# Clearing scratch words on GpSimd between the row gathers of a graph layer

## The chip, the cores and the metric

The kernel runs on one core of one Trainium2 chip. The metric is the device time of one execution in microseconds (us). The kernel before takes 2163.11 us, the median of three runs (2162.38, 2163.11 and 2164.73).

Engines are named as the profile names them: PE is TensorE's matmul side and PEld its weight load, DVE is VectorE, ACT is ScalarE, POOL is GpSimd, SP is SyncE. A trailing q (POOLq, SPq) is the engine's sequencer, which reads the instructions and tests their waits.

## The reference

`x` is 12500 x 256 float32; `src` and `dst` are 200000 edges, sorted by `dst`. The layer is

```python
h   = maximum(layernorm(x), 0)
agg = segment_sum(h[src], dst, 12500)
z   = (1 + eps_gin) * h + agg
t   = relu(batchnorm(z @ W1 + b1))          # 256 -> 512
y   = relu(batchnorm(t @ W2 + b2 + h))      # 512 -> 256
out = x + y
```

Both batch norms take mean and variance over all 12500 nodes, so nothing of the second product can start before the first product of every node is done.

## The kernel before

The edges are cut into 1563 tiles of 128 (the last has 64), and the tiles into 131 groups of `GT = 12` (the last group has 3). The nodes are cut into 25 chunks of 512. The kernel holds two programs, `fast()` and `general()`, and chooses by a flag; with these inputs it runs `fast()`.

**The gathers.** For each tile of 128 edges one indirect DMA, issued by GpSimd at line 513 in `gather(i)`, fetches 128 rows of 256 float32 (1 KB each) by the row numbers in `srcT`. Groups 0 to 29 fetch from `x` and are normalised on chip; from `LEAD = 30` on they fetch from `h_tab`, the normalised table that the kernel has written to DRAM meanwhile. Groups 0 and 1 are gathered ahead of the loop at line 238. A group's twelve gathers are issued from its last tile to its first: `for t in reversed(range(t0, t0 + n))`.

**The step.** One pass of the loop at line 726 is a step. Step `i` issues `gather(i + AHEAD)` with `AHEAD = 3` on GpSimd, so that three further groups are under way while group `i` is consumed. On VectorE `edges` (line 545) builds the one-hot matrices of a group; on TensorE `sums(i)` (line 570) multiplies twelve gathered tiles with them into one 128 x 256 sum, `put` (line 635) places an earlier group's sum in its columns of `zc`, and `slice_of` (line 661) is a quarter of the first product for a chunk whose edges are all in. The matmuls of a step are tied together by `together`, so that TensorE raises its semaphore once for them all. The order is written out by hand; each engine runs its own instructions in that order and waits on semaphores for the others.

**What a gather waits for.** Completed gathers are counted on eight semaphores in turn, so gather `n` waits for the landing of gather `n - 8`. The first gather of a group also waits for TensorE's step, which frees the buffer it writes into. The sequencer carries that second wait as an event-semaphore instruction of its own.

**After the last gather.** GpSimd does four small subtractions (lines 870 to 873). The kernel then closes the last sums, merges the statistics (line 288), runs the second product (lines 915, 944 and 952), the second batch norm and the way out. In that part GpSimd has some additions on 128 x 1024 (lines 936, 1008, 1014), and no gather is left.

**Other work of GpSimd.** At the very start it clears four constants of one word a partition, `dstT` and `srcT` beyond their filled part (lines 204 and 205, 91 words a partition), and the scratch tile `first` (lines 224 and 225), and writes index ramps with `iota` (lines 103 and 232 to 234).

Of the kernel before, what the change touches and what calls it, by code (L numbers as in the profile page):

```python
# [8 lines left out]
F32 = mybir.dt.float32  # L9
# [6 lines left out]
P = 128  # L16
R = 4
EPS = 1e-5
GT = 12
# [17 lines left out]
def kernel(  # L37
# [16 lines left out]
    nc = tc.nc  # L54
    N, D = x.shape
# [77 lines left out]
    def slot(ga, t):  # L133
        return slots(ga, t)[:, 0, :]
# [209 lines left out]
    def fast():  # L344
# [24 lines left out]
        with ExitStack() as fs:  # L369
# [14 lines left out]
            with ExitStack() as es:  # L384
                ln = es.enter_context(tc.tile_pool(name="ln", bufs=2))
                ring = es.enter_context(tc.tile_pool(name="ring", bufs=RING))
                sel = es.enter_context(tc.tile_pool(name="sel", bufs=2))
# [17 lines left out]
                relative(dstT, start)  # L405
                nc.vector.tensor_scalar(shift, shift, row, None, op0=OP.add)

                moments, scaled = {}, {}

                def look(v, pairs, tag, k):  # L410
# [93 lines left out]
                def gather(i):  # L504
                    t0, n = groups[i]
                    k = i % (AHEAD + 1)
                    if i >= LEAD + AHEAD or k > AHEAD - RING:
                        ga = ((0, GT, ring.tile([P, GT, D], F32, name="gt")),)
                    else:
                        ga = early[k]  # L510
                    for t in reversed(range(t0, t0 + n)):
                        rows = left if t == full_tiles else P
                        nc.gpsimd.indirect_dma_start(  # L513
                            out=slot(ga, t - t0)[:rows], out_offset=None, in_=x if i < LEAD else h_tab,
                            in_offset=bass.IndirectOffsetOnAxis(ap=srcT[:rows, t : t + 1], axis=0),
                        )
                    gathered[i] = ga

                def span(i):
# [188 lines left out]
                for i in range(EARLY, min(AHEAD, NG)):  # L708
                    gather(i)
# [16 lines left out]
                for i in range(NG - CLOSE):  # L726
                    before = added
                    gather(i + AHEAD)
                    if 0 < i <= NCH:
                        turn(i - 1)  # L730
# [50 lines left out]
                for i in range(NG - CLOSE, NG + 1):  # L781
                    if i + AHEAD < NG:
                        gather(i + AHEAD)
# [558 lines left out]
    with tc.If(off == 0):  # L1342
        fast()
# [32 lines left out]
```

## Time and profile before

| | us |
|---|---|
| median of 3 runs | 2163.11 |
| the profiled execution, its own time | 2162.41 |
| its span | 2160.5 |
| POOL busy | 1553.6 (72%) |
| PE busy | 1633.1 (76%) |
| DVE busy | 784.2 (36%) |
| ACT busy | 499.8 (23%) |

The profile is one execution of the program. Its span runs from the first instruction to the end of the last; the profiled execution's own time is 1.9 us above the span and 0.7 us below the median.

Groups of instructions read: line, engine, operation, output tile `<-` input tiles, count `|` busy time in us, mean ns of one `|` idle time of the engine just before them and what ended most of it. "issue" stands for time in which the engine waited for nothing that the profile shows. A timeline row reads: start in us, duration in us, engine, line, operation, and in brackets the idle time before it with what ended it. A row of the windows reads: the stretch, its length, the busy time of PE, PEld, DVE, ACT and POOL with the count of instructions, the clock granted to TensorE as a share of full speed, the mean busy share of the 16 DMA engines, and the GB/s moved. A row of the waits reads: the waiting engine and line, what ended the wait, the total in us, how often, the longest.

### The profile page before, as it was taken

Reading aid. Unit: us, or ns where it says so; the run is one execution under the profiler, and the core shown is the slowest. Engines: PE = TensorE matmul, PEld = TensorE weight load, DVE = VectorE, ACT = ScalarE, POOL = GpSimd, SP = SyncE. Lnnn points to the kernel's source line nnn. Section 1 sums busy time; section 2 is a strip of 40 time slices with the busy share of each in tenths; the row PEclk is TensorE's granted clock in tenths of the full one; section 3 lists DMA queues with packets and bytes.
Section 4 is the critical chain, followed back from the end, with each engine's and each line's share of the span. In section 5 each row is a group of like instructions: output and inputs, shape, how many; then the busy total and the mean of one; then the engine's idle time right before and its main releaser. Section 6 shows DMA issues by size and latency. Waiting matters only on the chain.

```text
span 2160.5 us, 15155 instructions
## 1 busy us (share of the span) xinstructions
PE 1633.1 (76%) x4856; PEld 987.2 (46%) x4856; DVE 784.2 (36%) x1172; ACT 499.8 (23%) x947; POOL 1553.6 (72%) x1609
## 2 busy tenths in 40 slices
PE   2666776778877777777777777778777777889997
PEld 2554554554444434444444444434444444455445
DVE  6565666542122121221212212122122122126997
ACT  4766667530000000000000000000000000004555
POOL 7777777777777777777777777777777777774540
PEclk9778888887788788887888878888788897789999
DMA  6766776644444444444444344444444445456898
GB/s 185 232 214 213 248 224 206 200 134 120 125 130 121 122 130 120 129 124 120 130 125 134 114 125 133 117 124 125 124 130 130 115 127 160 124 169 206 309 321 329
DMA packets 146048, 349.48 MB, mean 162 GB/s; under 512 B 30696, under 2 KB 58468, under 8 KB 145958
## 3 DMA queue, kind: packets, MB, share of 16 engines
q0 software_dynamic: 75008, 204.90, 33.4%
q1 hardware_dynamic: 43088, 104.47, 13.8%
q10 hardware_dynamic: 27862, 39.03, 5.0%
q8 instruction: 41, 0.67, 0.1%
q14 instruction: 49, 0.40, 0.1%
HBM read 284.28 MB, written 64.00 MB: 161 GB/s over the span
## 4 chain that ended last, share of the span: by engine, by line
POOL 54%; issue 23%; PE 8%; DMA 7%; DVE 5%; ACT 3%; SPq 0%; DVEq 0%; ACTq 0%; POOLq 0%
POOL gt L513 52%; DMA gt<-in_x_dram,srcT 4%; PE one L915 2%; PE pr L915 2%; PE pq L915 2%; ACT gt L441 1%; DMA gta<-in_x_dram,srcT 1%; DVE oh L545 1%; DVE stg L417 1%; DVE stc L417 1%; DMA gt<-h_tab,srcT 1%; POOL gta L238 1%; POOL gta L513 1%; ACT ht L441 1%; PE ps L570 0%
## 5 line engine op out<-in xcount | busy, mean ns | idle before, releaser
L513 POOL DMA_INDIRECT gt<-h_tab,srcT x1191 | 1125.8, 945 | 362.8 <-issue 362.2
L570 PE MATMUL ps<-gt,oh 128*128 128x256 f32 x2856 | 1001.4, 480 | 342.1 <-DMA gt<-h_tab,srcT 323.1
L570 PEld LDWEIGHTS ps<-gt,oh 128*128 128x128 f32 x2856 | 576.9, 226 | 765.1 <-DMA gt<-h_tab,srcT 662.2
L675 DVE BATCH_NORM_STATS2 st<-ph 128x6 f32<-128x512 f32 x96 | 67.0, 698 | 910.7 <-PE ph L661 910.7
L513 POOL DMA_INDIRECT gt<-in_x_dram,srcT x252 | 238.2, 945 | 76.8 <-issue 70.4
L621 ACT COPY zs<-ps 128x256 f32<-128x256 f32 x129 | 47.3, 367 | 804.9 <-PE ph L661 550.3
L545 DVE TENSOR_TENSOR oh<-col,dstT 128x1536 f32<-128x1536 f32 x129 | 225.1, 1746 | 0.0
L661 PE MATMUL ph<-zc,w1s 128*128 128x512 f32 (+1 forms) x392 | 206.3, 655 | 14.7 <-DVE hc L498 13.2
L681 ACT COPY ts<-ph 128x512 f32<-128x512 f32 x96 | 56.2, 586 | 590.3 <-DVE st L675 584.8
L651 DVE TENSOR_TENSOR zc<-pz,zc 128x512 f32<-128x512 f32 (+7 forms) x185 | 90.9, 517 | 258.1 <-PE pz L635 258.1
L635 PE MATMUL pz<-at,zs 128*128 128x256 f32 x516 | 170.7, 465 | 3.2 <-DVE zc L651 1.9
L635 PEld LDWEIGHTS pz<-at,zs 128*128 128x128 f32 x516 | 125.9, 245 | 31.2 <-ACT zs L621 5.2
L441 ACT ACTIVATE gt<-gt,nbg,rsg 128x256 f32<-128x256 f32 x252 | 126.1, 586 | 24.8 <-DVE nbg L435 24.8
L484 PE MATMUL ph<-ident,ht 128*128 128x128 f32 x196 | 44.0, 379 | 110.8 <-ACT ht L441 81.7
L661 PEld LDWEIGHTS ph<-zc,w1s 128*128 128x128 f32 x392 | 87.6, 225 | 83.9 <-issue 60.4
L417 DVE BATCH_NORM_STATS2 stg<-gt 128x6 f32<-128x512 f32 x126 | 84.4, 696 | 101.5 <-DMA gt<-in_x_dram,srcT 101.2
L484 PEld LDWEIGHTS ph<-ident,ht 128*128 128x128 f32 x196 | 31.1, 191 | 131.3 <-ACT ht L441 89.4
L513 POOL DMA_INDIRECT gta<-in_x_dram,srcT x56 | 52.9, 945 | 17.0 <-ACT gt L441 6.7
L626 DVE TENSOR_SCALAR at<-col,shift 128x256 f32<-128x256 f32 x129 | 61.2, 476 | 0.0
L936 POOL TENSOR_TENSOR ax<-ax,by 128x1024 f32<-128x1024 f32 x10 | 23.9, 2393 | 48.6 <-ACT by L893 44.7
L441 ACT ACTIVATE ht<-xt,nbc,rsc 128x256 f32<-128x256 f32 x98 | 50.5, 585 | 0.0
L570 PE MATMUL ps<-gtb,oh 128*128 128x256 f32 x80 | 31.9, 567 | 22.7 <-ACT gtb L441 22.2
(188 smaller groups left out, 1077.2 us busy)
## 6 DMA issues: line engine op xcount, KB each, us to landing
t_tab<-ts ACTq DMA_DIRECT2D x96, 256.0 KB
gt<-h_tab,srcT POOLq DMA_INDIRECT x1191, 2.8
xt<-in_x_dram SPq DMA_DIRECT2D x24, 512.0 KB
h_tab<-ht ACTq DMA_DIRECT2D x24, 512.0 KB
h_cols<-hc SPq DMA_DIRECT2D x24, 512.0 KB
zc<-h_cols SPq DMA_DIRECT2D x24, 512.0 KB
yT<-h_cols SPq DMA_DIRECT2D x24, 512.0 KB
ax<-t_tab SPq DMA_DIRECT2D x11, 512.0 KB
```

Of the source, the lines that this page charges most:

```text
L417: nc.vector.bn_stats(st[:, c : c + 2, :].rearrange("p c s -> p (c s)"), two.rearrange("p c d -> p d c"),)
L441: nc.scalar.activation(slot(to, c), slot(v, c), AF.Relu, bias=nb[:, c : c + 1], scale=rs[:, c : c + 1])
L484: nc.tensor.transpose(ph[:, c * P : (c + 1) * P], ht[:, c, d * P : (d + 1) * P], ident)
L513: nc.gpsimd.indirect_dma_start(out=slot(ga, t - t0)[:rows], out_offset=None, in_=x if i < LEAD else h_tab, in_offset=bass.IndirectOffsetOn ...
L545: nc.vector.tensor_tensor(ohs[i][:, :n, :], col[:, :P].unsqueeze(1).to_broadcast([P, n, P]), dstT[:, t0 : t0 + n].unsqueeze(2).to_broadcas ...
L570: nc.tensor.matmul(ps, lhsT=oh[:rows, j, :], rhs=slot(ga, j)[:rows], start=(j == order[0]), stop=(j == order[-1]))
L626: nc.vector.tensor_scalar(ats[i][:, :n], col[:, :n], shift[:, i : i + 1], None, op0=OP.is_equal)
L635: nc.tensor.matmul(pz[:, d, :n], lhsT=zs[:, d * P : (d + 1) * P], rhs=at[:, :n], start=True, stop=True)
L651: nc.vector.tensor_add(side, pz[:, :, a - lo : b - lo], side)
L661: nc.tensor.matmul(ph[:, :n], lhsT=w1s[:, d, f * P : (f + 1) * P], rhs=zc[c][:, d, :n], start=(d == 0), stop=(d == DC - 1),)
L675: nc.vector.bn_stats(st1[:, f, c, :], ph[:, :n])
L915: nc.tensor.matmul(ps, lhsT=w[:, k, :], rhs=t[:, k, :], start=(k == 0), stop=(k == DC - 1))
```

## The change

A scratch tile `gap` of 2048 float32 a partition is added. In 70 of the 131 groups GpSimd clears some of its words right after a gather, in five stretches of 14 groups each. Nothing reads `gap`.

| groups | words a partition | after which gathers | clearings |
|---|---|---|---|
| 50 to 63 | 83 | every one | 168 |
| 64 to 77 | 180 | every one | 168 |
| 78 to 91 | 327 | every one | 168 |
| 92 to 105 | 512 | tiles 8, 4 and 0 of the twelve | 42 |
| 106 to 119 | 2048 | tile 0, the last issued | 14 |

```diff
+                gap = sel.tile([P, 8 * D], F32, name="gap", bufs=1)
+                breaks = {}
+                for i0, long, every in ((50, 83, 1), (64, 180, 1), (78, 327, 1), (92, 2 * D, 4), (106, 8 * D, GT)):
+                    for i in range(i0, i0 + 14):
+                        breaks[i] = long, every
+
                 moments, scaled = {}, {}
...
                             out=slot(ga, t - t0)[:rows], out_offset=None, in_=x if i < LEAD else h_tab,
                             in_offset=bass.IndirectOffsetOnAxis(ap=srcT[:rows, t : t + 1], axis=0),
                         )
+                        if i in breaks and (t - t0) % breaks[i][1] == 0:
+                            nc.gpsimd.memset(gap[:, : breaks[i][0]], 0.0)
                     gathered[i] = ga
```

In the built program these are 560 clearings. Each but the first waits on GpSimd's own semaphore for the clearing before it, since both write the same words. No gather gets a new wait. The instructions of the other engines and their order are the same, but for one: a late load into `yT`, issued by SP, also waits for GpSimd, because that tile takes over the place of `gap`.

## The prediction

> **What bounds the kernel now.** I read the page first (chain and groups), then the waits and the windows of the loop's middle, then GpSimd's timeline at three places.
>
> ```profile
> span 2160.5 us, 15155 instructions
> ...
> POOL 54%; issue 23%; PE 8%; DMA 7%; DVE 5%; ACT 3%; SPq 0%; DVEq 0%; ACTq 0%; POOLq 0%
> ...
> L513 POOL DMA_INDIRECT gt<-h_tab,srcT x1191 | 1125.8, 945 | 362.8 <-issue 362.2
> ```
>
> The chain that ended last is POOL for 54% and "issue" for 23%. The group says that this issue time is GpSimd's own: between two gathers it is idle for 362.8 / 1191 = 0.305 us and waits for nothing that the profile names. A gather is 0.945 + 0.305 = 1.25 us. The waits from 800 to 1800 us agree:
>
> ```profile
> POOL gt L513 <- issue: 243.7, 800, 0.3
> POOL gt L513 <- DMA gt<-h_tab,srcT: 0.3, 1, 0.3
> ...
> PE ps L570 <- DMA gt<-h_tab,srcT: 237.3, 343, 2.5
> ```
>
> Of 800 gathers one waited for a landing, and none for TensorE to free a buffer. TensorE waits for gathers, 237.3 us of these 1000. So whatever GpSimd loses here is not made up by others: everyone else is waiting for it already.
>
> ```profile
> 40.00:400.00 360.00, 236.62 (x906) 185.07 (x907) 223.67 (x408) 243.73 (x511) 272.28 (x289) 0.82 0.69 217
> ...
> 1036.00:1246.00 210.00, 157.74 (x436) 89.66 (x435) 44.77 (x57) 12.95 (x26) 158.82 (x169) 0.84 0.42 123
> ...
> 1957.00:2160.50 203.50, 186.70 (x596) 99.91 (x594) 175.64 (x227) 107.30 (x143) 74.32 (x34) 0.97 0.83 300
> ```
>
> The second row stands for the changed stretches: 210 us hold 14 groups of 12 gathers, PE is busy 157.7 of them, the DMA engines 42%. The third is the part behind the last gather, 203.5 us in which nothing is gathered.
>
> ```profile
> 1953.23 0.90 POOL L513 DMA_INDIRECT gt<-h_tab,srcT  x1 [0.30 <-issue]
> 1954.44 0.95 POOL L513 DMA_INDIRECT gt<-h_tab,srcT  x1 [0.31 <-issue]
> 1955.70 0.95 POOL L513 DMA_INDIRECT gt<-h_tab,srcT  x1 [0.30 <-issue]
> 1958.84 0.72 POOL L870 TENSOR_TENSOR mix<-w2s 128x256 f32<-128x256 f32 x1 [2.19 <-PE ps L613]
> ```
>
> The gathers run from 3.21 us to 1956.65 us (1955.70 + 0.95) at an even 1.25 us, 1563 of them, and everything behind hangs on the last. A microsecond added between gathers is a microsecond on the end.
>
> **The change, part by part.** It removes nothing. It adds 168 + 168 + 168 + 42 + 14 = 560 clearings on GpSimd, and their waits.
>
> *The price of a clearing.* None stands between gathers before; the nearest rows are GpSimd's clearings at the start.
>
> ```profile
> 0.24 0.10 POOL L1362 MEMSET const-float32-0.0<- 128x1 f32 x1 [0.24 <-issue]
> 0.27 0.11 POOL L1362 MEMSET const-float32-1.0<- 128x1 f32 x1
> 0.30 0.12 POOL L1362 MEMSET const-bfloat16-1.0<- 128x1 bf16 x1
> 0.33 0.12 POOL L1362 MEMSET const-uint8-127<- 128x1 uint8 x1
> 0.85 0.23 POOL L103 IOTA jp<- 128x128 int32 x1 [0.40 <-POOLq L1362]
> 1.02 0.17 POOL L204 MEMSET dstT<- 128x91 f32 x1
> 1.14 0.17 POOL L205 MEMSET srcT<- 128x91 int32 x1
> 1.25 0.28 POOL L224 MEMSET first<- 128x128 f32 x1
> 1.49 0.24 POOL L232 IOTA place<- 128x131 int32 x1
> 1.67 0.19 POOL L225 MEMSET first<- 1x128 f32 x1
> 3.21 1.10 POOL L238 DMA_INDIRECT gtb<-in_x_dram,srcF  x1 [0.97 <-DMA srcF<-in_src_dram]
> 4.62 0.95 POOL L238 DMA_INDIRECT gtb<-in_x_dram,srcE  x1 [0.30 <-issue]
> 5.87 0.95 POOL L238 DMA_INDIRECT gtb<-in_x_dram,srcE  x1 [0.30 <-issue]
> ```
>
> These rows overlap each other (0.24 + 0.10 lies beyond 0.27), so I count from end to end, which is what the engine is held for. The one-word clearings end at 0.34 and 0.45, three steps apart: 0.037 us each. The two of 91 words end at 1.31, behind the ramp that ends at 1.08: 0.115 us each. That makes 0.037 us plus (0.115 - 0.037) / 90 = 0.867 ns a word. The 128-word clearing of one partition took 1.86 - 1.73 = 0.13 us, where the line gives 0.148. That one waited for the clearing of `first` with a ramp in between, much as the new ones wait, and shows no surcharge. So 83 words cost 0.109 us, 180 words 0.193, 327 words 0.320, 512 words 0.481 and 2048 words 1.812. The last two are far beyond the rows; at the 0.73 ns a word of the one-partition clearing the long ones would cost 0.411 and 1.53 us.
>
> Taken by the durations of the rows (0.1125 us for one word in the mean of four, 0.17 us for 91, so 0.64 ns a word), the five are 0.165, 0.227, 0.321, 0.439 and 1.42 us, and the sum below would be 168 x 0.713 + 42 x 0.439 + 14 x 1.42 = 158 us instead of 150. The Trainium skill, page "Perfetto Trace Analysis", section "GPSIMD Engine Instruction", says to distrust a GpSimd row's span and to time by the spacing of consecutive instructions; the overlapping rows here agree, and I go by the spacing.
>
> *Is the clearing hidden by something?* The candidate is the 0.305 us between gathers. If that were the sequencer making the next gather ready, the cores would stand still and could clear meanwhile. Sequencer rows speak against it (860 to 880 us, with the first gathers of a group):
>
> ```profile
> L513 POOLq EVENT_SEMAPHORE  x1: 17/17/17, 866.0 to 866.0; - x1
> ...
> DMA to landing us min/median/max: 2.7/2.8/4.4
> ```
>
> ```profile
> 873.30 0.95 POOL L513 DMA_INDIRECT gt<-h_tab,srcT  x1 [0.30 <-issue]
> 874.55 0.95 POOL L513 DMA_INDIRECT gt<-h_tab,srcT  x1 [0.30 <-issue]
> 875.80 0.95 POOL L513 DMA_INDIRECT gt<-h_tab,srcT  x1 [0.30 <-issue]
> ```
>
> The gather at 873.30 is number 1 + (873.30 - 4.62) / 1.25 = 696, counted from 0, which is 58 x 12, the first of group 58. It alone of its group has the extra wait, and the sequencer tested that at 866.0, 7.3 us or six gathers earlier. So gathers stand ready long before their turn, and the 0.305 us belongs to the engine's own work on a gather. Clearings then add in full. I take that, and keep the hidden case as a rival.
>
> *The waits of the clearings.* A clearing waits for the one before it, with at least one gather between. Behind it on the sequencer stand the next gathers, so the lead of six shrinks to about one. One is enough: the gather ahead holds the cores for 1.25 us, and the earlier clearing ended before that gather began. I cost this at 0; without that cover each of the 559 waits would show as part of a gather's 1.25 us. The gathers' own waits gain slack: eight gathers take 10 us or more against landings of 2.8 (4.4 at most), and TensorE frees its buffers relative to a slower pace.
>
> *VectorE beside it.* The 128-word clearing of 128 partitions took 1.53 - 1.31 = 0.22 us, 0.07 more than the line. VectorE was busy at that moment. In the stretches VectorE is busy 44.8 of 210 us: if every clearing met it by that share, 560 x 0.21 x 0.07 = 8 us. I leave that in the range.
>
> *The wait of SP.* One `yT` load waits for the last clearing, which lies 11 groups, some 150 us, before the last gather; these loads come behind the gathers. Cost 0.
>
> *The sum.* 168 x (0.109 + 0.193 + 0.320) + 42 x 0.481 + 14 x 1.812 = 104.5 + 20.2 + 25.4 = 150 us. The profiled execution would be 2162.4 + 150 = 2312.4 (span 2310.5); the median is 0.7 above it, so I forecast 2313 us. What is late next: nothing new, TensorE only waits longer. Its lower load might raise the granted clock, but behind the gathers that stands at 0.97, so at most 3% of 186.7, 5.6 us, could be won there.
>
> **The rivals.**
>
> *The gap hides them.* If the cores really rest in the 0.305 us, 83 and 180 words are free, 327 cost 0.015, 512 cost 0.176 and 2048 cost 1.507: 168 x 0.015 + 42 x 0.176 + 14 x 1.507 = 31 us, or 2194. For it: the profile can't name the gap. Against it: the lead of six gathers.
>
> *A gather behind a clearing starts cold.* The first gather, the only one behind other GpSimd work, took 1.10 instead of 0.95, and the next followed 1.41 us after it instead of 1.25. If each of 560 gathers paid 0.16, that is 90 more: 2403. For it: that row. Against it: it was also the first gather of all, and no later row separates the two.
>
> *The pace is the transfers'.* If the DMA path, not GpSimd, set 1.25 us, GpSimd would have slack in every gather, clearings up to it would be free, and after a long one it would catch up: 2163, not slower. The point that decides is whether a gather still follows 1.25 us after the one before in the first stretch. For it: the 64-row gather (the row at 1953.23) held its place for 1.21 us, hardly less than one of 128. Against it: the pace is the same with the DMA engines at 69% (40 to 400 us) and at 42%, and one gather's landing takes 2.8 us with several in flight. With a higher clock behind the gathers on top this could even end some us faster.
>
> That the clearings aren't carried out is hardly open: all 560 stand in the program.
>
> **How the numbers follow.** Full cost 0.72; cold restarts 0.12; hidden in the gap 0.11; pace of the transfers 0.05, of which 0.01 faster. The forecast is the first case, 2313. Its own range is 2285 to 2340: the cheaper slope takes 42 x 0.07 + 14 x 0.28 = 7 us off, a hidden 0.037 us per clearing another 21; VectorE adds 8, and the 158 us of the durations as much again. The range of 8 in 10 takes in the cold restarts and leaves the two hidden cases out: 2280 to 2403. Slower by over 0.2% (4.3 us, about what a measurement of this kernel can tell from no change) holds all but the last case: slower 0.95, same 0.04, faster 0.01.
>
> **What the changed profile would show.** GpSimd's timeline should have gathers 1.36, 1.44 and 1.57 us apart in the first three stretches, in the fourth 1.25 with 1.73 across each clearing, in the fifth 1.25 with 3.06; the five stretches 228, 242, 264, 230 and 235 us long instead of 210. TensorE's waits for gathers should grow by as much, and the part behind the last gather stay near 203.5 us. A spacing of 1.25 in the first two stretches shows the gap or the transfers at work, and the long clearing tells them apart: followed by gathers closer than 1.25, it is the transfers. Gathers of 1.10 behind clearings show the cold restart. The prediction is wrong as a whole if the long clearings' slope is far from 0.87 ns, or if the shrunken lead lets gathers wait by name.

## The result and the profile after

The changed kernel takes 2276.73 us (median of three runs, 2276.61 to 2276.80) against 2163.11 before: a ratio of 1.0524, 95% interval 1.0500 to 1.0548. It is 113.6 us slower. The forecast was 150 us more, with a range that began at 2280. The direction and the place were right; the price of one clearing was too high.

The page of the changed kernel, its chain and its groups on GpSimd (`gather` is now at line 519, the clearing at 524):

```profile
span 2274.9 us, 15716 instructions
...
POOL 63%; issue 18%; PE 8%; DMA 5%; DVE 3%; ACT 2%; POOLq 0%; ACTq 0%; DVEq 0%
...
L519 POOL DMA_INDIRECT gt<-h_tab,srcT x1191 | 1129.8, 949 | 286.1 <-issue 285.2
...
L524 POOL MEMSET gap<- 128x83 f32 (+4 forms) x560 | 188.7, 337 | 0.3
```

The chain has more of POOL and less of "issue". The clearings are 188.7 us of busy time, but the idle time before the gathers fell from 362.8 to 286.1 us. The 560 clearings took a part of that idle time, and this is most of the miss. In the timeline one sees it at a single clearing of the first, third and fifth stretch:

```profile
759.97 0.95 POOL L519 DMA_INDIRECT gt<-h_tab,srcT  x1 [0.16 <-issue]
760.92 0.18 POOL L524 MEMSET gap<- 128x83 f32 x1
761.27 0.95 POOL L519 DMA_INDIRECT gt<-h_tab,srcT  x1 [0.16 <-issue]
...
1441.06 0.95 POOL L519 DMA_INDIRECT gt<-h_tab,srcT  x1 [0.17 <-issue]
1442.01 0.38 POOL L524 MEMSET gap<- 128x327 f32 x1
1442.56 0.95 POOL L519 DMA_INDIRECT gt<-h_tab,srcT  x1 [0.17 <-issue]
...
1697.13 0.95 POOL L519 DMA_INDIRECT gt<-h_tab,srcT  x1 [0.30 <-issue]
1698.38 0.95 POOL L519 DMA_INDIRECT gt<-h_tab,srcT  x1 [0.30 <-issue]
1699.32 1.82 POOL L524 MEMSET gap<- 128x2048 f32 x1
1701.31 0.95 POOL L519 DMA_INDIRECT gt<-h_tab,srcT  x1 [0.17 <-issue]
```

A clearing begins as the gather ends, with no gap. Behind it the next gather starts after 0.165 us, not after the 0.305 that stand between two gathers (0.30 in the last stretch, where two gathers adjoin). So 0.14 us of the gap stand between two gathers alone. The rows of the five sizes, by their forms, give the clearing's own length:

```profile
L524 POOL MEMSET gap<- 128x327 f32 x168 | 65.0, 387 | 0.1
...
L524 POOL MEMSET gap<- 128x180 f32 x168 | 44.4, 265 | 0.1
L524 POOL MEMSET gap<- 128x83 f32 x168 | 30.9, 184 | 0.1
...
L524 POOL MEMSET gap<- 128x2048 f32 x14 | 25.5, 1825 | 0.0
...
L524 POOL MEMSET gap<- 128x512 f32 x42 | 22.8, 543 | 0.0
```

That is 0.115 us plus 0.833 ns a word (0.387 - 0.184 over 244 words). The 0.14 us cover the 0.115 and 0.025 more; against that, the gather behind a clearing shows a longer row, 0.952 us in place of 0.946. Together this is 0.115 - 0.140 + 0.006 = -0.019 us for each clearing, beside its words. What is left on the path is seen in the spacing of gathers, start to start, as the median of a stretch; beside it what the stretches lengthened by:

| words, after which gathers | spacing without / with a clearing, us | one clearing costs | forecast | stretch longer by | forecast |
|---|---|---|---|---|---|
| 83, each | 1.250 / 1.299 | 0.049 | 0.109 | 8.8 | 18.3 |
| 180, each | 1.250 / 1.380 | 0.130 | 0.193 | 22.1 | 32.4 |
| 327, each | 1.250 / 1.502 | 0.252 | 0.320 | 43.1 | 53.8 |
| 512, every fourth | 1.250 / 1.650 | 0.400 | 0.481 | 17.1 | 20.2 |
| 2048, every twelfth | 1.250 / 2.930 | 1.680 | 1.812 | 23.6 | 25.4 |

The five points lie on one line, 0.833 ns a word less 0.019 us, within 0.008 us; divided by the number of clearings, the stretches lie within 0.004 us of it. So the distance between clearings does not seem to enter. The stretches sum to 114.7 us and the span grew by 114.4.

The windows of the changed kernel, the five stretches and the part behind the last gather:

```profile
753.47:972.33 218.86, 161.33 (x437) 92.67 (x436) 45.49 (x60) 13.63 (x27) 190.50 (x337) 0.83 0.42 121
972.33:1204.44 232.11, 180.98 (x436) 101.45 (x436) 45.36 (x58) 14.57 (x28) 204.12 (x336) 0.74 0.39 112
1204.44:1457.58 253.14, 192.10 (x433) 101.96 (x433) 44.82 (x58) 13.98 (x27) 224.59 (x336) 0.70 0.36 104
1457.58:1684.62 227.04, 175.28 (x436) 98.23 (x437) 45.49 (x60) 13.63 (x27) 181.73 (x210) 0.77 0.41 117
1684.62:1918.16 233.54, 172.55 (x436) 93.03 (x435) 44.76 (x57) 13.98 (x27) 184.33 (x183) 0.80 0.39 111
2071.40:2274.90 203.50, 187.12 (x598) 100.37 (x596) 176.18 (x227) 107.40 (x143) 74.20 (x35) 0.97 0.83 301
```

The last row is as before: 203.5 us, clock 0.97. Nothing was won or lost behind the gathers.

### The profile page after: what moved, and what is told of

The parts are those of the page before. It is cut to its first block, busy times and chain, and to the rows that moved or that the text cites. A ratio compares the mean times of both kernels' runs of the same rounds, so it can differ in the third digit from the quotient of the medians.

```text
span 2274.9 us, 15716 instructions
## 1 busy us (share of the span) xinstructions
PE 1713.9 (75%) x4856; PEld 1023.0 (45%) x4856; DVE 784.5 (34%) x1172; ACT 499.8 (22%) x947; POOL 1744.7 (77%) x2169
## 4 chain that ended last, share of the span: by engine, by line
POOL 63%; issue 18%; PE 8%; DMA 5%; DVE 3%; ACT 2%; POOLq 0%; ACTq 0%; DVEq 0%
POOL gt L519 53%; POOL gap L524 8%; DMA gt<-in_x_dram,srcT 3%; PE one L923 2%; ACT gt L447 2%; PE pr L923 2%; PE pq L923 2%; DMA gta<-in_x_dram,srcT 1%; DVE oh L553 1%; POOL gta L519 1%; ACT ht L447 1%; PE pq L952 1%; POOL gta L238 1%; DVE stg L423 1%; DVE stc L423 0%
## 5 line engine op out<-in xcount | busy, mean ns | idle before, releaser
L519 POOL DMA_INDIRECT gt<-h_tab,srcT x1191 | 1129.8, 949 | 286.1 <-issue 285.2
L578 PE MATMUL ps<-gt,oh 128*128 128x256 f32 x2856 | 1058.2, 501 | 378.3 <-DMA gt<-h_tab,srcT 360.6
L578 PEld LDWEIGHTS ps<-gt,oh 128*128 128x128 f32 x2856 | 598.5, 236 | 836.3 <-DMA gt<-h_tab,srcT 733.8
L519 POOL DMA_INDIRECT gt<-in_x_dram,srcT x252 | 238.2, 945 | 76.8 <-issue 71.3
L669 PE MATMUL ph<-zc,w1s 128*128 128x512 f32 (+1 forms) x392 | 213.7, 675 | 15.5 <-DVE hc L504 13.9
L524 POOL MEMSET gap<- 128x83 f32 (+4 forms) x560 | 188.7, 337 | 0.3
L643 PE MATMUL pz<-at,zs 128*128 128x256 f32 x516 | 184.6, 496 | 3.2 <-DVE zc L659 1.9
L643 PEld LDWEIGHTS pz<-at,zs 128*128 128x128 f32 x516 | 133.4, 259 | 34.4 <-ACT zs L629 5.5
L669 PEld LDWEIGHTS ph<-zc,w1s 128*128 128x128 f32 x392 | 92.6, 238 | 89.6 <-issue 63.9
L519 POOL DMA_INDIRECT gta<-in_x_dram,srcT x56 | 52.9, 945 | 17.1 <-issue 8.2
L944 POOL TENSOR_TENSOR ax<-ax,by 128x1024 f32<-128x1024 f32 x10 | 23.6, 2361 | 46.7 <-ACT by L901 39.7
```

The costliest lines, as they stand in the source:

```text
L519: nc.gpsimd.indirect_dma_start(out=slot(ga, t - t0)[:rows], out_offset=None, in_=x if i < LEAD else h_tab, in_offset=bass.IndirectOffsetOn ...
L524: nc.gpsimd.memset(gap[:, : breaks[i][0]], 0.0)
L578: nc.tensor.matmul(ps, lhsT=oh[:rows, j, :], rhs=slot(ga, j)[:rows], start=(j == order[0]), stop=(j == order[-1]))
L643: nc.tensor.matmul(pz[:, d, :n], lhsT=zs[:, d * P : (d + 1) * P], rhs=at[:, :n], start=True, stop=True)
L669: nc.tensor.matmul(ph[:, :n], lhsT=w1s[:, d, f * P : (f + 1) * P], rhs=zc[c][:, d, :n], start=(d == 0), stop=(d == DC - 1),)
```

## The experiments

All spacings below are medians of gather starts in the trace, without a stretch's first and last group. The first four kernels ran on one chip beside the kernel before (2166.13 us there); each replaces the five stretches by eight of ten groups, groups 40 to 119.

**How small may a clearing be?**

```diff
-                for i0, long, every in ((50, 83, 1), (64, 180, 1), (78, 327, 1), (92, 2 * D, 4), (106, 8 * D, GT)):
-                    for i in range(i0, i0 + 14):
-                        breaks[i] = long, every
+                for k, long in enumerate((1, 8, 16, 24, 36, 48, 64, 128)):
+                    for i in range(40 + 10 * k, 50 + 10 * k):
+                        breaks[i] = long
...
+                        if i in breaks:
+                            nc.gpsimd.memset(gap[:, : breaks[i]], 0.0)
```

> One clearing after every gather, in eight stretches of ten groups (groups 40 to 119) of 1, 8, 16, 24, 36, 48, 64 and 128 words a partition. The changed kernel's five stretches lie on one line: a clearing lengthens the spacing of two gathers by 0.833 ns a word minus 0.019 us. Theory of room: beside a gather there are 0.056 us in which a clearing runs free, and the clearing itself is 0.037 us plus 0.833 ns a word; then the spacing stays at 1.250 us for 1, 8 and 16 words and grows by 0.001, 0.011, 0.021, 0.034 and 0.088 us for the others; together 120 x 0.155 = 19 us. Rival, replacement: a gather that follows another instruction is 0.019 us shorter than one that follows a gather, so the line goes on below zero: 1 word -0.018 us, 8 words -0.012, 16 words -0.006, and the others as above; together 120 x 0.119 = 14 us, and the kernel with one word everywhere would be the fastest. Rival, the prediction's own: 0.037 us at one word, 0.144 at 128.

| words | 1 | 8 | 16 | 24 | 36 | 48 | 64 | 128 |
|---|---|---|---|---|---|---|---|---|
| spacing, us | 1.251 | 1.257 | 1.257 | 1.257 | 1.257 | 1.264 | 1.277 | 1.333 |

The kernel takes 2184.64 us, 18.5 more than before. GpSimd's rows at 24 and at 128 words:

```profile
1119.98 0.95 POOL L519 DMA_INDIRECT gt<-h_tab,srcT  x1 [0.17 <-issue]
1120.92 0.14 POOL L524 MEMSET gap<- 128x24 f32 x1
1121.23 0.95 POOL L519 DMA_INDIRECT gt<-h_tab,srcT  x1 [0.17 <-issue]
...
1732.53 0.95 POOL L519 DMA_INDIRECT gt<-h_tab,srcT  x1 [0.16 <-issue]
1733.48 0.22 POOL L524 MEMSET gap<- 128x128 f32 x1
1733.86 0.95 POOL L519 DMA_INDIRECT gt<-h_tab,srcT  x1 [0.16 <-issue]
```

There is a floor. One word is free, and from 8 to some 36 words a clearing costs 0.006 us, by which the gather behind it shows a longer row (0.952 in place of 0.946). Replacement falls: one word does not shorten the spacing, and 8 and 16 words lengthen it. The prediction's price falls too: it makes 120 x 0.578 = 69 us of these 325 words. The theory of room holds in kind, but its sizes are off by 0.004 to 0.007 us, too low from 8 to 24 words and too high from 36 on, so that its sum of 19 us meets the 18.5 in part by luck. The time alone could not tell 19 from 14: both kernels ran once on this chip, and three runs of the kernel before lie 2.4 us apart.

**Is the room there once for each gap?**

```diff
+                gaps = [sel.tile([P, 2 * D], F32, name=f"gap{k}", bufs=1) for k in range(4)]
+                for k, longs in enumerate(((180,), (90, 90), (60, 60, 60), (45, 45, 45, 45), (1, 1), (1, 1, 1, 1), (180, 1), (1, 180))):
...
+                        for gap, long in zip(gaps, breaks.get(i, ())):
+                            nc.gpsimd.memset(gap[:, :long], 0.0)
```

> The clearing after each gather cut up, each piece in a tile of its own, in eight stretches of ten groups: 180 words; 2 x 90; 3 x 60; 4 x 45; 2 x 1; 4 x 1; 180 and 1; 1 and 180. Room once for each gap between gathers (0.056 us, each clearing 0.037 us plus 0.833 ns a word): spacing grows by 0.131, 0.168, 0.205, 0.242, 0.020, 0.094, 0.169 and 0.169 us. Rival, a clearing has no fixed cost at all and the words alone count, less 0.019 us once: 0.131 in the first four, 0 in the two with single words, 0.131 to 0.132 in the last two.

| pieces | 180 | 2 x 90 | 3 x 60 | 4 x 45 | 2 x 1 | 4 x 1 | 180, 1 | 1, 180 |
|---|---|---|---|---|---|---|---|---|
| spacing, us | 1.380 | 1.413 | 1.439 | 1.472 | 1.251 | 1.296 | 1.413 | 1.408 |

The kernel takes 2294.69 us. A further clearing in the same gap costs 0.026 to 0.033 us beside its words. So a clearing has a fixed price, somewhat below the 0.037 forecast, and the room is there once for each gap: the rival without a fixed price falls. The two stretches of single words do not fit the theory: with two the spacing is 1.251, as the fallen rival had it, where 1.270 was expected, and with four 1.296, where 1.344 was. In the trace a further single word starts 0.028 us after the one before, as dear as a further clearing elsewhere and not the 0.038 of the theory, so that two of them just fit the room. With four, the next gather starts 0.151 us behind the last and not 0.163; why stays open.

**Which partitions hold GpSimd?**

```diff
+                for k, part in enumerate(((0, 128, 512), (0, 32, 512), (32, 64, 512), (64, 128, 512), (0, 1, 512), (64, 128, 1024), (64, 128, 2048), (0, 128, 1024))):
...
+                            p0, p1, long = breaks[i]
+                            nc.gpsimd.memset(gap[p0:p1, :long], 0.0)
```

> One clearing after every gather over a part of the partitions, in eight stretches of ten groups: partitions 0 to 127 x 512 words, 0 to 31 x 512, 32 to 63 x 512, 64 to 127 x 512, partition 0 x 512, 64 to 127 x 1024, 64 to 127 x 2048, 0 to 127 x 1024. If the engine is held by the instruction whatever its partitions: 0.41 us more spacing in the first five, 0.83, 1.69 and 0.83 in the others. If only the cores that prepare a gather are held, and these own low partitions: 0.41, 0.41, about 0, about 0, 0.41, about 0 for 1024 words, and for 2048 words, which are longer than a gather's 1.25 us, a spacing of about 1.75 set by the clearings themselves (0.5 more); 0.83 in the last.

| partitions x words | 0-127 x 512 | 0-31 x 512 | 32-63 x 512 | 64-127 x 512 | 0 x 512 | 64-127 x 1024 | 64-127 x 2048 | 0-127 x 1024 |
|---|---|---|---|---|---|---|---|---|
| spacing, us | 1.657 | 1.657 | 1.657 | 1.657 | 1.625 | 2.083 | 2.937 | 2.084 |

```profile
1698.63 0.95 POOL L519 DMA_INDIRECT gt<-h_tab,srcT  x1 [0.16 <-issue]
1699.57 0.98 POOL L525 MEMSET gap<- 64x1024 f32 x1
1700.71 0.95 POOL L519 DMA_INDIRECT gt<-h_tab,srcT  x1 [0.16 <-issue]
```

The kernel takes 2806.64 us. The engine is held by the instruction, whatever its partitions. The Trainium skill, page "GPSIMD Engine Reference", section "2.1 Instruction dispatch", says that each core begins the next instruction once its own share is done, and section "4. When to use GPSIMD" that one pair of cores prepares a DMA. From these one could hope that clearing partitions 64 to 127 leaves that pair free. These runs show no such thing: 64 partitions cost what 128 do, and so do partitions 0 to 31 and 32 to 63. These three parts share no partition, so whichever pair it is, one of them holds none of it. Only one partition alone is cheaper, by 0.032 us.

**Waits, distance, and other instructions.**

```diff
+                gaps = [sel.tile([P, D], F32, name=f"gap{k}", bufs=1) for k in range(7)]
+                ramp = sel.tile([P, D], I32, name="ramp", bufs=1)
+                for k, kind in enumerate((("one", 1), ("seven", 1), ("ramp", 1), ("one", 2), ("one", 3), ("one", 6), ("one", 12), ("copy", 1))):
...
+                                nc.gpsimd.memset(gaps[t % 7][:, :180], 0.0)
...
+                                nc.gpsimd.iota(ramp[:, :180], pattern=[[1, 180]], base=0, channel_multiplier=0)
...
+                                nc.gpsimd.tensor_copy(gaps[1][:, :180], gaps[0][:, :180])
```

> 180 words a partition in eight stretches of ten groups: cleared in one tile after every gather; in seven tiles in turn, so that a clearing waits for one seven gathers back; an index ramp in place of the clearing; the clearing after every 2nd, 3rd, 6th and 12th gather; a copy from one scratch tile to another after every gather. If the waits between clearings cost nothing, the first two are alike, 0.131 us more spacing. If the price of a clearing does not depend on the distance, each costs 0.131 us at every distance. If the saving belongs to the gather that follows anything else, ramp and copy show the same one: their own words' time less about 0.02 us (0.83 to 1.0 ns a word: 0.13 to 0.16 us); if it belongs to the clearing, they cost about 0.04 to 0.06 us more than that.

The kernel takes 2259.07 us. One tile and seven tiles in turn give 1.380 us each: the waits between clearings cost nothing. Nor does the sequencer's lead matter: it tests a group's first gather 1.5 us ahead with one tile and 8.2 us ahead with seven. At every 2nd, 3rd, 6th and 12th gather the spacing across a clearing is 1.373 us and the next one up to 0.006 longer, and a clearing lengthens its stretch by 0.126 to 0.132 us at every distance, so the price does not depend on it. The ramp gives 1.411, the copy 1.490. At the program's start a ramp of only 131 words took 0.20 us from end to end (1.73 less 1.53); here one of 180 adds 0.160, so there is room beside a ramp too, at least 0.04 us. The rows say the same of both: the next gather starts 0.161 us behind a ramp and 0.167 behind a copy, as behind a clearing. The copy's 0.239 us more lie outside both expectations. Its own row is longer (0.341 us, against 0.262 of a clearing), and so is the gather behind it (0.977).

**Short clearings, the same words in fewer clearings, and VectorE.** Three kernels were meant to show the room in the time itself.

```diff
+                for i0, long, every in ((50, 24, 1), (64, 24, 1), (78, 24, 1), (92, 24, 4), (106, 24, GT)):
```

> The changed kernel with all its 560 clearings at their places, but of 24 words a partition each. Theory of room: a spacing of 1.257 us where one stands, 0.006 to 0.007 more, so 3 to 4 us in all, about 2166.5 us beside 2163. The prediction's price (0.037 us plus 0.867 ns a word, all of it on the path): 560 x 0.058 = 32 us, about 2195.

```diff
+                for i0, long, every in ((50, 12 * 83, GT), (64, 6 * 180, 6), (78, 6 * 327, 6), (92, 6 * D, GT), (106, 8 * D, GT)):
```

> The words of the changed kernel, 149,296 a partition over each stretch as there, in 98 clearings in place of 560: 996 words once a group, 1080 twice, 1962 twice, 1536 once, 2048 once. Theory of room: the room beside a gather is used 98 times in place of 560, so 149,296 x 0.833 ns less 98 x 0.019 us = 122.5 us, about 2286: fewer clearings are slower by some 9 us than the changed kernel's 2276.7. If each clearing has a price of its own of 0.037 us, as predicted, fewer clearings are faster, by 462 x 0.037 = 17 us: about 2260.

```diff
+                breaks = {i: (180, 1) for i in range(6, 26)}
```

> 180 words after every gather of groups 6 to 25 alone, where VectorE is busy 62% of the time in place of 21%. If VectorE does not matter: 0.131 us more spacing, 240 x 0.131 = 31 us more in all. If it holds clearings up as the prediction's bound had it, 0.07 us for a share of 0.62 of them: 0.17 us more spacing, 42 us. If GpSimd is not what sets the pace there, less than 31 us at the end.

They came to another chip, and there the kernel before took 2463.8 us. So they ran again on two further chips, with the changed kernel beside them.

> The kernel with 560 clearings of 24 words once more, on a chip where the kernel before takes about 2163 us if one is given. Where GpSimd sets the pace: 560 x 0.006 us = 3 to 4 us more than before. Where TensorE stalls set the pace, as in the run before: no difference that can be measured.

> The same words in 98 clearings once more. Where GpSimd sets the pace: about 122 us more than before, some 9 us more than the changed kernel beside it. Where TensorE stalls set the pace: 0 to 20 us more, and no order against the changed kernel that could be told.

> The changed kernel itself beside the other two on one chip. Where GpSimd sets the pace: 113 to 114 us more than before, as measured. Where TensorE stalls set the pace: far less, since GpSimd then waits for TensorE in any case and a clearing falls into that wait.

> 180 words after every gather of groups 6 to 25 once more. Where GpSimd sets the pace: spacing 1.380 us there and 31 us more at the end. In the run before the spacing was 1.38 us and the end within 3 us of the kernel before.

> 560 clearings of 24 words, where GpSimd sets the pace: 560 x 0.006 us = 3 to 4 us more than before (theory of room); 560 x 0.058 = 32 us more (the prediction's price).

> The same words in 98 clearings, where GpSimd sets the pace: 122.5 us more than before and 9 us more than the changed kernel (theory of room); 17 us less than the changed kernel (a price of its own for each clearing).

> The changed kernel beside the other two on one chip: 113 to 114 us more than before where GpSimd sets the pace.

> 180 words after every gather of groups 6 to 25, where GpSimd sets the pace: spacing 1.380 us there and 31 us more at the end if VectorE does not matter; 42 us if it holds clearings up.

| us; ratio to before, 95% interval | first chip | second | third |
|---|---|---|---|
| before | 2463.8 | 2464.7 | 2455.7 |
| 24 words | 2452.9; 0.9971 (0.9932 to 1.0009) | 2468.6; 1.0016 (0.9996 to 1.0036) | 2456.6; 1.0009 (0.9989 to 1.0030) |
| same words, 98 clearings | 2471.8; 1.0048 (1.0004 to 1.0092) | 2482.1; 1.0072 (1.0049 to 1.0095) | 2472.2; 1.0078 (1.0052 to 1.0105) |
| changed kernel | | 2481.1; 1.0061 (1.0038 to 1.0085) | 2470.8; 1.0075 (1.0046 to 1.0103) |
| VectorE busy (one run) | 2466.2 | 2468.4 | 2460.5 |

On the two of these chips on which the changed kernel ran, the change costs 15 and 16 us in place of 114. The 24 words cost nothing that can be measured, and the 31 us expected of 180 words in groups 6 to 25 come out as 2 to 5, in single runs. TensorE's largest group in the changed kernel, as first measured and on the second chip, TensorE's rows on the second chip, and GpSimd's waits there from 753 to 1963 us, which is from before the first stretch into the fifth:

```profile
L578 PE MATMUL ps<-gt,oh 128*128 128x256 f32 x2856 | 1058.2, 501 | 378.3 <-DMA gt<-h_tab,srcT 360.6
```

```profile
L578 PE MATMUL ps<-gt,oh 128*128 128x256 f32 x2856 | 972.1, 471 | 532.0 <-issue 389.7
```

```profile
1167.77 0.38 PE L578 MATMUL ps<-gt,oh 128*128 128x256 f32 x1 [0.52 <-issue]
1169.16 0.38 PE L578 MATMUL ps<-gt,oh 128*128 128x256 f32 x1 [1.02 <-issue]
1170.60 0.58 PE L578 MATMUL ps<-gt,oh 128*128 128x256 f32 x1 [1.06 <-issue]
1172.02 0.58 PE L578 MATMUL ps<-gt,oh 128*128 128x256 f32 x1 [0.84 <-issue]
1173.45 0.79 PE L578 MATMUL ps<-gt,oh 128*128 128x256 f32 x1 [0.85 <-issue]
1176.25 1.29 PE L578 MATMUL ps<-gt,oh 128*128 128x256 f32 x2 [2.00 <-issue]
```

```profile
POOL gt L519 <- issue: 176.9, 824, 0.8
POOL gt L519 <- remote: 51.4, 15, 6.4
POOL gap L524 <- remote: 7.2, 7, 1.5
```

As first measured, TensorE's idle time was spent waiting for gathers; here most of it is "issue", and in such phases its rows start 1.4 and 2.8 us apart while it waits for nothing that the profile shows. GpSimd's gathers now have 15 waits of up to 6.4 us, whose releaser the profile can't name ("remote"). In the trace each wait of a gather over 0.9 us in the five stretches stands before the first gather of a group, the one that waits for TensorE's step. The lengths of the five stretches, from their first gather to the next stretch's, show which engine sets the pace (second chip / third chip):

| stretch | 24 words | changed kernel | same words, 98 clearings |
|---|---|---|---|
| 50 to 63 | 241.9 / 239.3 | 242.1 / 240.7 | 236.8 / 240.1 |
| 64 to 77 | 237.8 / 240.2 | 239.6 / 237.7 | 240.4 / 237.1 |
| 78 to 91 | 243.9 / 239.8 | 253.2 / 253.1 | 255.8 / 255.7 |
| 92 to 105 | 237.4 / 237.0 | 238.2 / 237.9 | 237.3 / 236.9 |
| 106 to 119 | 241.2 / 238.2 | 239.6 / 237.3 | 240.4 / 237.4 |

TensorE, by this account, needs some 238 us for 14 groups here: a stretch with 24 words lasts 237 to 244, where GpSimd's spacing alone would make it 211. A stretch of GpSimd that is shorter hides under it: 219, 232, 227 and 234 us do. Only the third, 253, is longer, and its 15 us are about the whole loss. In that stretch GpSimd sets the pace in both kernels, and there the sign comes out as the theory of room has it: the same words in 28 clearings take 2.6 us more than in 168. By the theory of room it is 28 x 1.615 - 168 x 0.252 = 2.9 us more; with the prediction's price it would have been 140 x 0.037 = 5 us less. In the whole time the two kernels can't be told apart on these chips, and the time of the 24-word kernel tests no price there.

The medians hold too: a gap with 24 words is 1.257 and 1.260 us, where gathers without clearings follow 1.251 and 1.254 apart, and 180 words in groups 6 to 25 give 1.380 to 1.383. VectorE is busy 54% of the time there in these runs (62% was expected). A clearing during which VectorE was busy for over nine tenths of its row costs the same as one that VectorE did not meet at all: the medians are 1.382 and 1.382, 1.383 and 1.383, 1.379 and 1.380 us on the three chips. So the VectorE work that stands beside the clearings has no part in the price. Why TensorE stalls on these chips was not tried.

## Why the prediction was wrong, point by point

- **GpSimd's gathers set the pace, and lost time is not made up.** Right. The stretches grew by 114.7 us, the span by 114.4, and the part behind the gathers stayed at 203.5.
- **"Clearings then add in full."** This step failed. The lead of the sequencer shows that gathers stand ready early, but not that the engine's 0.305 us keep another instruction out. They are two parts: 0.165 that stand before a gather behind a clearing, a ramp or a copy as well, and 0.14 that stand only between two gathers. In the latter a clearing runs free, which the floor at 1 to 36 words shows. What the engine does in these 0.14 us when a gather follows stays open. Set against the prediction's line, 0.056 us of each clearing vanish: the fixed 0.037, which stood in its own range as "a hidden 0.037 us per clearing", and 0.019 of its words. Over 560 clearings that is 31.4 of the 36 us missed.
- **The slope.** 0.867 ns a word came from two rows of 91 words and four of one word, at two decimals; it measured 0.833. Over 149,296 words that is 5 us.
- **The gap as a rival.** It came nearer the mechanism, but took the whole 0.305 us as free: it gives 31 us. The truth lay between both, and no case stood there; a range that reached from the full price down to this rival would have held the time. The first case's own range had the hidden 0.037 us in it and stopped at 2285, 8 us short. At its upper end the terms listed, 8 and 8 us, make 2329 and not 2340.
- **Durations against spacing.** By the rows' spans a clearing of 83 words is 0.184 us, by the spacing of gathers it costs 0.049. The Trainium skill's rule to go by spacing (page "Perfetto Trace Analysis", section "GPSIMD Engine Instruction") is borne out; the spacing taken, of clearings among themselves, was only not that beside a gather.
- **Cold restarts.** Fell: gathers behind clearings take 0.952 us, not 1.10.
- **The transfers' pace.** Fell: the gather behind the long clearing came 2.93 us after the one before, and those behind it 1.25 apart.
- **The waits of the clearings, VectorE, SP's load.** Cost nothing that shows. The lead shrank as forecast: in the first three stretches the sequencer tests a group's first gather 1.4 to 1.6 us ahead in place of 7.2. VectorE's 8 us, left in the range, did not come.
- **The signs of being wrong.** Neither came: the slope was 0.833 against 0.867 ns, and 285.2 of the 286.1 us before the gathers are still "issue". So these signs did not cover the step that failed. The spacings did, 1.30 in place of 1.36 us in the first stretch.
- **TensorE's waits and clock.** Wrong. Its waits for gathers should have grown by as much as the time. Over the five stretches, before (753 to 1803 us) and after (753 to 1918 us):

```profile
PE ps L570 <- DMA gt<-h_tab,srcT: 247.4, 356, 2.5
```

```profile
PE ps L578 <- DMA gt<-h_tab,srcT: 273.3, 390, 3.2
```

They grew by 26 us of 115. The granted clock fell in place of rising, and longer matmuls took up most of the rest: TensorE's busy time in these stretches went from 797 to 882 us. That cost nothing, since TensorE had slack.

## What to carry to other kernels

An idle gap between two instructions of one kind is not wholly the engine's, nor wholly free: part of it may belong to that pair alone, and another instruction can run in it. Price a short instruction where it will stand, and where no row shows that place, let the range reach from the full price to the whole gap. And a stretch costs what it lasts beyond the next slowest engine: the same clearings cost 114 us where GpSimd set the pace throughout, and 15 to 16 where only one of the five stretches outlasted the 238 us that TensorE seems to need.

## What the runs showed of the hardware that was not expected

The clock granted to TensorE falls where gathers are spaced further apart. In the same groups it was 0.83 before and 0.83 at a spacing of 1.30 us, 0.83 and 0.74 at 1.38, 0.80 and 0.70 at 1.50. After, these are the windows above; before, the same groups read:

```profile
753.30:963.30 210.00, 160.53 (x438) 90.27 (x436) 45.50 (x60) 13.65 (x27) 158.83 (x168) 0.83 0.43 127
963.30:1173.30 210.00, 160.48 (x437) 90.54 (x436) 45.36 (x58) 14.59 (x28) 158.86 (x168) 0.83 0.42 124
1173.30:1383.30 210.00, 160.80 (x432) 93.58 (x432) 44.83 (x58) 14.00 (x27) 158.83 (x168) 0.80 0.43 125
```

In the kernel that clears parts of the partitions, stretches at 1.66 and 2.94 us:

```profile
634.00:802.00 168.00, 124.31 (x256) 62.68 (x256) 25.16 (x32) 7.79 (x15) 151.26 (x204) 0.63 0.32 91
...
1880.00:2220.00 340.00, 167.48 (x310) 78.79 (x309) 32.52 (x42) 9.35 (x19) 320.65 (x239) 0.57 0.19 55
```

Four stretches at 1.63 to 1.66 us read 0.65 to 0.68 beside the 0.63 shown. TensorE's busy share does not fall with its clock in the first three stretches of the changed kernel: it is 0.74, 0.78 and 0.76 (161.33 of 218.86 us and so on), since matmuls grow longer. The Trainium skill, page "TensorE: Matmul & The Clock Gate", section "Part 1: The HAM clock gate (the "warmup" mystery)", says that the gate sets the clock by how busy the array has been of late. The rows agree in so far as less work a microsecond goes with a lower clock; what the gate counts as busy no run here shows.

The other thing is the chips: the kernel before, with the same inputs, took 2162 to 2166 us where it was first measured and on the chip of the first four experiments, and 2449 to 2479 in all 42 runs on three others. The kernels traced there show TensorE stalls in the loop that no view of the profile puts down to a wait.
